# A two-layer graph network on one core: the first block's rows gathered from x during the prologue

## The chip, the core and the metric

The kernel runs on one core of one Trainium2 chip. The metric is the device time of one execution in microseconds; the median of several runs is compared. A core has five engines that run beside each other, each with its own queue: TensorE (PE in the profile, its weight loads PEld), VectorE (DVE), ScalarE (ACT), GpSimd (POOL) and SyncE (SP). SP issues most of the plain loads and stores here; GpSimd issues the gathers (indirect DMAs).

## What is computed

Two message-passing layers over a graph of 6250 nodes and 200000 edges, sorted by destination. `x` has 128 features per node. Cut to what matters:

```python
h = relu(layernorm(x))
z = h @ W                                   # 128 features, as 8 heads of 16
el, er = z . attn_l, z . attn_r             # per head
e = leaky_relu(el[src] + er[dst], 0.2)
a = exp(e - segment_max(e, dst)[dst])
x = x + segment_sum(z[src] * a, dst) / segment_sum(a, dst) + bias

h = relu(layernorm(x))
s, v = h[:, :32] @ W_up_s, h[:, 32:] @ W_up_v
w = silu(silu(edge_attr_8 @ A1 + b1) @ A2 + b2) @ A3
m = products of s[src], v[src], edge_attr_4 and w       # 256 per edge
x = x + (segment_sum(m, dst) / 10) @ W_out
```

What bears on the change is `z[src]` and `el[src]`: each edge needs a row of 136 values (128 of `z`, 8 of `el`) of its source node. `layernorm`, relu and the product with `W` act on each row by itself, so a row of the table can be made from a row of `x`, wherever that row has been copied to.

## The kernel before

**The edges.** The edges are cut into tiles of 128 (1563 of them), and 16 tiles (`KB`) make a block; there are 98 blocks (`NB`). A block's edges fall into a window of 128 nodes, so sums over edges are products with one-hot matrices on TensorE.

**The prologue** (L842 to L957) makes the table `t0` in DRAM: one row of 136 values per node. The nodes are 50 tiles of 128 rows, in ten chunks `gx` of 2, 3, 5, 6, 6, 6, 6, 6, 6 and 4 tiles. SP loads the ten chunks of x (`xs`, L865), then `src_col` (the source of every edge), `d_i` and `q_i` (destinations of every edge and of the edge before it) and `off`. Then a software pipeline steps over the chunks: `moments` (mean and variance on DVE, L814 and L816), `deviation` (a square root on ACT, L821), `normal` (DVE, L826 and L828), the normalized tile `fh` (L895 on ACT, L899 on GpSimd or DVE), a transpose on PE (L909), relu on ACT (`h_t`, L911), the product with `w_ext` (L917), a copy to `zt` on ACT, or on DVE for the last two chunks (L922), and `to_table` (L785 to L798), which stores `zt` to `t0` by SP. The last 8 columns of the product, `er`, are copied to `er_all` on GpSimd (L926). PE, DVE and ACT run in the order in which the program is written (`manual_schedule`); SP and GpSimd in an order that the scheduler chooses.

After the chunks GpSimd gathers the 16 tiles of block 0 from `t0` into `z_first` (L833). DVE checks that the edges are in order and evenly spread (L933 to L950) and leaves a number in `ok_i`; `er_all` is split into three bf16 parts `er3` (L953 to L957). Each engine then loads `ok_i` (L958) and takes one of two branches (L959): `even_edges`, which runs here, or a general kernel.

**The branch** loads constants and weights by SP (L990 to L1011), makes masks over the edges (L1014 to L1050: DVE, ACT, and five loads by SP), and then runs layer 0 as a loop over the blocks, with PE, DVE, ACT and SP in the written order. GpSimd issues 16 gathers for each block, or 15 where SP fetches the last tile row by row (L1078, every third block). The gathered block lies in one of five buffers `g` of the pool `fz`; `take_rows(g + 3)` asks for a block three steps before it is used, and a buffer comes back when the block's sums (L1234, PE) are done. Block 0 uses `z_first`. Layer 1 runs in the same way from a second table; its gathers have the same form.

Of the kernel before, what the change touches and what calls it, by code (L numbers as in the profile page):

```python
# [9 lines left out]
F32 = mybir.dt.float32  # L10
BF = mybir.dt.bfloat16
I32 = mybir.dt.int32
AF = mybir.ActivationFunctionType
OP = mybir.AluOpType
AX = mybir.AxisListType
PSUM = bass.MemoryType.PSUM
DRAM = bass.MemoryType.DRAM

P = 128
H = 8  # L20
D = 16
F = H * D
ZW = F + H
# [6 lines left out]
KB = 16  # L30
# [705 lines left out]
W0 = 32  # L736
# [5 lines left out]
def tile_even_edges(  # L742
# [46 lines left out]
    def to_table(table, of, i, n, eng):  # L789

        if i == 0:
            eng.dma_start(table[: P - W0, :], of[W0:, 0, :])
            if n > 1:
                to = table[P - W0 : n * P - W0]
                eng.dma_start(to.rearrange("(j p) f -> p j f", p=P), of[:, 1:n, :])
            return
        to = table[i * P - W0 : (i + n) * P - W0]
        eng.dma_start(to.rearrange("(j p) f -> p j f", p=P), of[:, :n, :])  # L798
# [20 lines left out]
    def deviation(pool, mv, n, name, m=P):  # L819
        rs = pool.tile([P, n, 1], F32, name=f"rs{name}")  # L820
        nc.scalar.activation(rs[:m], mv[:m, :, 1:2], AF.Sqrt, bias=eps[:m])  # L821
        return rs

    def normal(pool, mv, rs, n, name, m=P):

        nc.vector.reciprocal(rs[:m], rs[:m])  # L826
        mr = pool.tile([P, n, 1], F32, name=f"mr{name}")
        nc.vector.scalar_tensor_tensor(mr[:m], mv[:m, :, 0:1], -1.0, rs[:m], op0=OP.mult, op1=OP.mult)  # L828
        return rs, mr
# [8 lines left out]
    def tiles_of(a, first):  # L838
        return a[first : first + TG * P * P].rearrange("(g t e) -> t g e", t=P, e=P)


    with tc.manual_schedule(engines={mybir.EngineType.PE, mybir.EngineType.DVE,  # L842
                                     mybir.EngineType.Activation}), \
# [12 lines left out]
        w_ext = fx.tile([P, CW], F32, name="fw_ext")  # L856
# [9 lines left out]
        nc.sync.dma_start(src_col, srcc)  # L866
        d_i = fx.tile([P, TG, P], I32, name="fd_i")
        nc.sync.dma_start(d_i, tiles_of(dstt, P))
        q_i = fx.tile([P, TG, P], I32, name="fq_i")
        nc.sync.dma_start(q_i, tiles_of(dstt, P - 1))  # L870
        off = fx.tile([P, TG], F32, name="foff")
        nc.sync.dma_start(off, nums[:, NB * KB : NB * KB + TG])
# [7 lines left out]
        er_all = fx.tile([P, NX, H], F32, name="fer_all")  # L880
        NC = len(gx)
        mvs, rss, mrs, hs = {}, {}, {}, {}
        todo, done, outs = [], [], []
        for k in range(NC + 3):
            if 0 <= k - 1 < NC:
                rss[k - 1] = deviation(fp, mvs[k - 1], gx[k - 1][1], f"x{gx[k - 1][0]}")
            c = k - 2
            if 0 <= c < NC:
                i, n = gx[c]
                rs, mr = rss[c], mrs[c] = normal(fp, mvs[c], rss[c], n, f"x{i}")  # L890
                h = hs[c] = fp.tile([P, 10, P], F32, name="fh")
                for j in range(n):
                    by = (i + j) % 7
                    if by in ((2, 6) if c < NC - 2 else (2,)):
                        nc.scalar.activation(h[:, j, :], xs[c][:, j, :], AF.Identity,  # L895
                                             bias=mr[:, j, :], scale=rs[:, j, :])
                    else:
                        eng = nc.gpsimd if by in (0, 3, 5) and c < NC - 2 else nc.vector
                        eng.tensor_scalar(h[:, j, :], xs[c][:, j, :], mvs[c][:, j, 0:1],  # L899
                                          rs[:, j, :], op0=OP.subtract, op1=OP.mult)  # L900
            if k >= 3:
                i, n = gx[k - 3]
                zt = fp.tile([P, 10, CW], F32, name="zt")
                todo += [(k - 3, zt, j0, min(3, n - j0)) for j0 in range(0, n, 3)]
            while todo:
                c, zt, j0, m = todo.pop(0)
                p_t = fp_ps.tile([P, 4, P], F32, name="p_t")
                for j in range(m):
                    nc.tensor.transpose(p_t[:, j, :], hs[c][:, j0 + j, :], ident)  # L909
                h_t = fp.tile([P, 3, P], F32, name="h_t")  # L910
                nc.scalar.activation(h_t[:, :m], p_t[:, :m], AF.Relu)  # L911
                done.append((c, zt, j0, m, h_t))
                while len(done) > (1 if k < NC + 2 or todo else 0):
                    c, zt, j0, m, h_t = done.pop(0)
                    p_z = fp_ps.tile([P, 3, CW], F32, name="p_z")
                    for j in range(m):
                        nc.tensor.matmul(p_z[:, j, :], h_t[:, j, :], w_ext, start=True, stop=True)  # L917
                    outs.append((c, zt, j0, m, p_z))
                    while len(outs) > (1 if k < NC + 2 or todo or done else 0):
                        c, zt, j0, m, p_z = outs.pop(0)  # L920
                        copy = nc.scalar.copy if c < NC - 2 else nc.vector.tensor_copy
                        copy(zt[:, j0 : j0 + m, :], p_z[:, :m])  # L922
                        i, n = gx[c]
                        if j0 + m == n:
                            to_table(t0, zt[:, :, :ZW], i, n, nc.sync)
                            nc.gpsimd.tensor_copy(er_all[:, i : i + n, :], zt[:, :n, ZW:])  # L926
            if k < NC:
                i, n = gx[k]
                mvs[k] = moments(fp, xs[k], n, f"x{i}")
        gather(z_first, t0, range(KB), ZW)  # L930

        bad = fx.tile([P, TG, P], F32, name="fbad")
        nc.vector.tensor_tensor(bad, d_i, q_i, OP.is_lt)  # L933
        vs = fx.tile([P, 4], F32, name="fvs")
        nc.vector.tensor_reduce(vs[:, 0:1], bad.rearrange("p g e -> p (g e)"), AX.X, OP.add)
        w3 = fx.tile([P, 3, TG], F32, name="fw3")
        ef = fx.tile([P, 2, TG], F32, name="fef")
        nc.vector.tensor_sub(ef[:, 0, :], d_i[:, :, 0], off)
        nc.vector.tensor_sub(ef[:, 1, :], d_i[:, :, P - 1], off)
        nc.vector.tensor_single_scalar(w3[:, 0, :], ef[:, 0, :], 0.0, op=OP.is_lt)  # L940
        nc.vector.tensor_single_scalar(w3[:, 1, :], ef[:, 1, :], float(P), op=OP.is_ge)
        nc.vector.tensor_tensor(w3[:, 2, :], ef[:, 0, :], ef[:, 1, :], OP.is_equal)
        nc.vector.tensor_reduce(vs[:, 1:2], w3.rearrange("p a g -> p (a g)"), AX.X, OP.add)
        ones = fx.tile([P, 1], F32, name="fones")
        nc.vector.memset(ones, 1.0)
        p_v = fp_ps.tile([P, 4, P], F32, name="p_t")
        nc.tensor.matmul(p_v[:1, 0, :2], ones, vs[:, :2], start=True, stop=True)
        vr = fx.tile([1, 1], F32, name="fvr")
        nc.vector.tensor_reduce(vr, p_v[:1, 0, :2], AX.X, OP.add)
        nc.vector.tensor_copy(ok_i, vr)  # L950
# [14 lines left out]
def even_edges(tc, v):  # L965
# [5 lines left out]
    xp, dstc, y4, f8, bias, out, moments, deviation, normal, gather, tiles_of = (v[k] for k in (  # L971
        "xp", "dstc", "y4", "f8", "bias", "out", "moments", "deviation", "normal", "gather", "tiles_of"))
    with ExitStack() as ctx:
        const = ctx.enter_context(tc.tile_pool(name="fconst", bufs=1))
        z_pool = ctx.enter_context(tc.tile_pool(name="fz", bufs=5))
# [22 lines left out]
        wup = const.tile([P, P], F32, name="fwup")  # L998
        nc.sync.dma_start(wup, v["wup"])
        a1p = const.tile([P, KB // 2, P], F32, name="fa1p")  # L1000
        nc.sync.dma_start(a1p, v["a1p"])
        a2p = const.tile([P, P], F32, name="fa2p")
        nc.sync.dma_start(a2p, v["a2p"])
        a3p = const.tile([P, 2, P], F32, name="fa3p")
        nc.sync.dma_start(a3p, v["a3p"])
        b1 = const.tile([P, 1], F32, name="fb1")
        nc.sync.dma_start(b1, v["b1"])
        b2 = const.tile([P, 1], F32, name="fb2")
        nc.sync.dma_start(b2, v["b2"])
        wout = const.tile([P, 2, P], F32, name="fwout")  # L1010
        nc.sync.dma_start(wout, v["wout"])  # L1011
# [11 lines left out]
        with tc.tile_pool(name="fbuild", bufs=1) as build:  # L1023
            d_c = build.tile([P, TU], I32, name="fd_c")
            nc.sync.dma_start(d_c, dstc)
            d_i = build.tile([P, TG, P], I32, name="fd_i")
            nc.sync.dma_start(d_i, tiles_of(dstt, P))
            q_i = build.tile([P, TG, P], I32, name="fq_i")
            nc.sync.dma_start(q_i, tiles_of(dstt, P - 1))
# [20 lines left out]
            nc.sync.dma_start(t1z[LATE * P - W0 :].rearrange("(j p) f -> p j f", p=P), zeros)  # L1050

# [796 lines left out]
```

## Time and profile before

| | us |
|---|---|
| median of three runs | 3887.06 (3886.89 to 3891.37) |
| profiled execution | 3888.67 |
| its span | 3886.9 |
| busy: GpSimd | 2913.0 (75%) |
| busy: TensorE matmuls | 2848.8 (73%) |
| busy: VectorE | 2224.5 (57%) |
| busy: ScalarE | 1396.8 (36%) |
| first gather into `fz_first` | starts at 42.58 |
| first gather of the branch (block 1) | starts at 63.16 |

The span is the time from the first to the last record of the profiled execution; 1.8 us of its own time lie around it. A line of the profile's groups reads: line of the program, engine, operation, output and inputs by name, count, then the busy time with the mean of one, then the idle time just before these instructions and what ended most of it. In the timeline a row has its start and its duration in us, and in square brackets the idle time before it and what ended that. A queue of an engine (SPq, POOLq) is its sequencer, which issues DMAs, waits on semaphores and takes branches.

### The profile page before, as it was taken

How to read it: one execution, taken by the hardware profiler on the slowest of the kernel's cores; microseconds unless marked ns; L12 is line 12 of the kernel's file. 1: busy time of each engine (PE TensorE's matmuls, PEld its weight loads, DVE VectorE, ACT ScalarE, POOL GpSimd, SP SyncE). 2: the span in 40 equal slices, each digit the busy share in tenths (PEclk: the TensorE clock that was granted, in tenths of full speed). 3: DMA queues.
4: the chain of work that ended last, by engine and by line, in shares of the span. 5: the costliest groups of instructions: out<-in, count | busy, mean ns of one | idle time of the engine just before them, and what ended most of it. 6: DMA issues, size and time to landing. Idle time of an engine off the chain costs nothing. (4 is left out here: it accounts for less than half of the span.)

```text
span 3886.9 us, 62701 instructions
## 1 busy us (share of the span) xinstructions
PE 2848.8 (73%) x14785; PEld 2401.2 (62%) x14785; DVE 2224.5 (57%) x5408; ACT 1396.8 (36%) x3612; POOL 2913.0 (75%) x3096
## 2 busy tenths in 40 slices
PE   3766666666666766666678888888877777778777
PEld 3656656656556656666666666666666556656665
DVE  5544444444444444444457777677766666666666
ACT  3323232323322323232324444444444444444443
POOL 6777777777777777777777777777777777777776
PEclk6666666666666566666689999999999999999999
DMA  6222222222222222222222222222222222222221
GB/s 181 59 64 64 62 64 64 64 62 64 62 64 62 64 61 64 62 64 62 61 61 61 61 62 62 62 62 62 62 62 62 62 62 61 63 60 63 61 61 50
DMA packets 195262, 252.65 MB, mean 65 GB/s; under 512 B 78656, under 2 KB 145088, under 8 KB 194880
## 3 DMA queue, kind: packets, MB, share of 16 engines
q0 software_dynamic: 98048, 207.27, 22.6%
q1 hardware_dynamic: 96544, 41.19, 4.1%
q8 instruction: 120, 1.97, 0.2%
q14 instruction: 262, 2.15, 0.2%
q10 hardware_dynamic: 288, 0.07, 0.0%
HBM read 234.73 MB, written 13.25 MB: 64 GB/s over the span
## 5 line engine op out<-in xcount | busy, mean ns | idle before, releaser
L833 POOL DMA_INDIRECT g<-ft,fsrc x3024 | 2856.7, 945 | 922.4 <-issue 858.3
L1570 PE MATMUL p_u<-mj,s 128*128 128x256 f32 x3126 | 789.9, 397 | 217.9 <-DVE mj L1562 216.5
L1570 PEld LDWEIGHTS p_u<-mj,s 128*128 128x128 f32 x3126 | 588.9, 196 | 385.7 <-DVE mj L1562 310.9
L1234 PE MATMUL p_u<-g,s 128*128 128x136 f32 x3062 | 597.8, 376 | 0.4 <-DVE g L1229 0.4
L1234 PEld LDWEIGHTS p_u<-g,s 128*128 128x128 f32 x3062 | 572.1, 279 | 0.5 <-DVE g L1229 0.4
L1537 ACT ACTIVATE p_w<-p_w,yb 128x64 f32<-128x64 f32 x1563 | 450.3, 288 | 121.5 <-PE p_w L1533 80.4
L1553 DVE TENSOR_TENSOR vy<-g,p_i 128x384 f32<-128x384 f32 x387 | 212.9, 550 | 366.6 <-DMA g<-ft,fsrc 258.0
L1533 PE MATMUL p_w<-fa3p,h 128*128 128x256 f32 x1564 | 412.0, 387 | 0.0
L1151 PE MATMUL p_d<-fident,s 128*128 128x128 f32 x1563 | 384.7, 411 | 0.0
L1533 PEld LDWEIGHTS p_w<-fa3p,h 128*128 128x128 f32 x1564 | 289.4, 195 | 118.1 <-issue 52.5
L1176 DVE TENSOR_TENSOR e_s<-g,p_n 128x128 f32<-128x128 f32 x96 | 27.5, 286 | 578.6 <-DMA g<-ft,fsrc 566.2
L1518 ACT ACTIVATE h<-p_h,fb 128x512 f32<-128x512 f32 x196 | 134.6, 687 | 573.2 <-PE p_h L1516 571.8
L1151 PEld LDWEIGHTS p_d<-fident,s 128*128 128x128 f32 x1563 | 312.4, 225 | 37.6 <-issue 26.3
L1144 ACT COPY mk<-p_m 128x385 f32<-128x385 f32 (+1 forms) x99 | 47.6, 481 | 781.3 <-PE p_m L1141 781.2
L1229 DVE TENSOR_TENSOR g<-g,pe 128x1024 f32<-128x1024 f32 x193 | 225.5, 1209 | 129.2 <-ACT g L1220 126.4
L1153 ACT CAST d<-p_d 128x512 bf16<-128x512 f32 x391 | 228.8, 586 | 192.0 <-PE p_d L1151 141.6
L1179 PE MATMUL pe<-fident,e_s 128*128 128x128 f32 x98 | 39.1, 399 | 326.2 <-DVE e_s L1177 326.2
L1097 DVE TENSOR_TENSOR s<-p_n,fdloc 128x512 f32<-128x512 f32 x391 | 266.1, 682 | 6.7 <-ACT sv L1289 3.4
L1097 DVE TENSOR_TENSOR s<-p_i,fdloc 128x512 f32<-128x512 f32 x391 | 266.1, 681 | 3.8 <-ACT p_i L1512 3.8
L1516 PE MATMUL p_h<-ft,fa1p 128*128 128x128 f32 x1568 | 217.2, 283 | 63.3 <-DMA ft<-in_e_f_dram 63.1
L1516 PEld LDWEIGHTS p_h<-ft,fa1p 128*128 128x128 f32 x1568 | 210.6, 198 | 83.9 <-issue 65.3
L1523 ACT ACTIVATE h<-p_h,fb 128x512 f32<-128x512 f32 x196 | 134.7, 687 | 307.1 <-PE p_h L1520 307.1
(202 smaller groups left out, 3344.3 us busy)
## 6 DMA issues: line engine op xcount, KB each, us to landing
r<-ft SPq DMA_DIRECT2D x3968, 0.5 KB
r<-ft SPq DMA_DIRECT2D x3968, 0.5 KB
g<-ft,fsrc POOLq DMA_INDIRECT x3024
ft<-in_e_f_dram SPq DMA_DIRECT2D x98, 64.0 KB
yb<-in_e_y_dram SPq DMA_DIRECT2D x98, 32.0 KB
fx_all<-in_e_xp_dram SPq DMA_DIRECT2D x48, 64.0 KB
out_dram<-fx_all SPq DMA_DIRECT2D x47, 64.0 KB
ft<-sv SPq DMA_DIRECT2D x46, 64.0 KB
```

The costliest lines, as they stand in the source:

```text
L833: nc.gpsimd.indirect_dma_start(out=to[:, k, :width], out_offset=None, in_=table, in_offset=bass.IndirectOffsetOnAxis(ap=src_col[:, t : t + ...
L1097: nc.vector.tensor_tensor(s[:, :m], iota[:, None, :].to_broadcast([P, m, P]), dloc[:, t : t + m].unsqueeze(2).to_broadcast([P, m, P]), OP. ...
L1151: nc.tensor.transpose(p_d[:, k, :], c["s"][q][:, k, :], ident)
L1153: nc.scalar.copy(d[:, :m], p_d[:, :m])
L1229: nc.vector.tensor_mul(zh, zh, p_a[:, k0 : k0 + m].unsqueeze(3).to_broadcast([P, m, H, D]))
L1234: nc.tensor.matmul(c["p_u"][:, :ZW], c["s"][k // 4][:, k % 4, :], c["z"][:, k, :], start=c["o"] + k == 0, stop=c["o"] + k == KT[c["b"]] - 1)
L1516: nc.tensor.matmul(p_h[:, q, :], a1p[:, q0 + q, :], c["ft"], start=True, stop=True)
L1523: nc.scalar.activation(h2, p_h, AF.Silu, bias=b2)
L1533: nc.tensor.matmul(w[:, k : k + n].rearrange("p k a u -> p (k a u)"), c["h2"][q // 4][:, q % 4, :], a3p[:, :n].rearrange("p k f -> p (k f) ...
L1537: nc.scalar.activation(w[:, k, ::2, :], w[:, k, ::2, :], AF.Copy, scale=c["yb"][:, k0 + k, 0:1])
L1553: nc.vector.tensor_mul(vy, v_n, y_p)
L1570: nc.tensor.matmul(blk[b]["p_u"][:, :MW], u["s"][:, k, :], u["mj"][:, k, :], start=k0 + k == 0, stop=k0 + k == KT[b] - 1)
```

## The change

- The scheduler's freedom in the prologue ends: GpSimd and SP follow the written order too.
- GpSimd gathers 16 x 128 rows of `x` (not of the table) into `z_first` at the beginning of the prologue. Their indices are the first 16 columns of the sources, loaded by themselves as `src_0` on ACT's queue, plus 32 for the padding of `x`.
- The pipeline over chunks becomes a function `rows_of`. It is called a second time in the branch, after the masks, on `z_first` in chunks of 6, 6 and 4 tiles; there its result is written over `z_first` itself. The gathers of `z_first` from `t0` are gone. `w_ext` moves to the pool that outlives the prologue.
- In the prologue GpSimd normalizes only in chunks 6 and 7 (5 tiles; before, 17 tiles in all). The others go to DVE, and so do the copies to `er_all`.
- `off`, `d_i` and `src_col` are loaded later: after the store of chunk 1 (`off`, `d_i`) and of chunk 3 (`src_col`). One load with 129 values per row stands for `d_i` and `q_i`, here and in the branch. `zt` has four buffers of six tiles for three of ten.
- The check of the edges is cut in two: the comparisons run on DVE one step before the last chunk (`uneven_edges`), the count as bf16 products on PE with one reduction (`count_uneven`).
- In the branch the pool `fz` is opened before `fconst`, and the masks and the pass over `z_first` stand ahead of the loads of the weights of layer 1.

The diff, cut to its core:

```diff
@@ prologue
     with tc.manual_schedule(engines={mybir.EngineType.PE, mybir.EngineType.DVE,
-                                     mybir.EngineType.Activation}), \
+                                     mybir.EngineType.Activation, mybir.EngineType.Pool,
+                                     mybir.EngineType.SP}), \
...
-        w_ext = fx.tile([P, CW], F32, name="fw_ext")
+        src_0 = fx.tile([P, KB], I32, name="fsrc0")
+        nc.scalar.dma_start(src_0, srcc[:, :KB])
+        w_ext = keep.tile([P, CW], F32, name="fw_ext")
...
-        nc.sync.dma_start(src_col, srcc)
-        d_i = fx.tile([P, TG, P], I32, name="fd_i")
-        nc.sync.dma_start(d_i, tiles_of(dstt, P))
-        q_i = fx.tile([P, TG, P], I32, name="fq_i")
-        nc.sync.dma_start(q_i, tiles_of(dstt, P - 1))
-        nc.sync.dma_start(off, nums[:, NB * KB : NB * KB + TG])
+        def load(k):
+            if k == 1:
+                nc.sync.dma_start(off, nums[:, NB * KB : NB * KB + TG])
+                nc.sync.dma_start(d_i, with_before(dstt))
+            elif k == 3:
+                nc.sync.dma_start(src_col, srcc)
...
+        row_0 = fx.tile([P, KB], I32, name="frow0")
+        nc.vector.tensor_single_scalar(row_0, src_0, W0, op=OP.add)
+        for k in range(KB):
+            nc.gpsimd.indirect_dma_start(
+                out=z_first[:, k, :P], out_offset=None, in_=xp,
+                in_offset=bass.IndirectOffsetOnAxis(ap=row_0[:, k : k + 1], axis=0))
...
+        def uneven_edges():
+            nc.vector.tensor_tensor(bad, d_i[:, :, 1:], d_i[:, :, :P], OP.is_lt)
...
+        def count_uneven():
+            p_v = fp_ps.tile([P, 512], F32, name="p_v", bufs=1)
+            b = bad.rearrange("p g e -> p (g e)")
+            for k in range(0, TG * P, 512):
+                n = min(512, TG * P - k)
+                nc.tensor.matmul(p_v[:1, :n], ones, b[:, k : k + n], start=k == 0, stop=False)
+            nc.tensor.matmul(p_v[:1, : 3 * TG], ones, w3.rearrange("p a g -> p (a g)"),
+                             start=False, stop=True)
+            vr = fx.tile([1, 1], F32, name="fvr")
+            nc.vector.tensor_reduce(vr, p_v[:1, :], AX.X, OP.add)
+            nc.vector.tensor_copy(ok_i, vr)
+
+        def rows_of(gx, xs, raw, fp, fp_ps):
...
-                        eng = nc.gpsimd if by in (0, 3, 5) and c < NC - 2 else nc.vector
+                            late = by in (0, 3, 5) and NC - 4 <= c < NC - 2 and not raw
+                            eng = nc.gpsimd if late else nc.vector
...
+                if k == NC + 1 and not raw:
+                    uneven_edges()
+                for i, n, zt in ers:
+                    nc.vector.tensor_copy(er_all[:, i : i + n, :], zt[:, :n, ZW:])
+                ers = []
                 if k >= 3:
                     i, n = gx[k - 3]
-                zt = fp.tile([P, 10, CW], F32, name="zt")
+                    zt = z_first[:, i : i + n, :] if raw else fp.tile([P, 6, CW], F32, name="zt", bufs=4)
...
-                            to_table(t0, zt[:, :, :ZW], i, n, nc.sync)
-                            nc.gpsimd.tensor_copy(er_all[:, i : i + n, :], zt[:, :n, ZW:])
+                            if j0 + m == n and not raw:
+                                to_table(t0, zt[:, :, :ZW], i, n, nc.sync)
+                                ers.append((i, n, zt))
+                                load(c)
...
-        gather(z_first, t0, range(KB), ZW)
+        rows_of(gx, xs, "", fp, fp_ps)
+        count_uneven()
@@ even_edges
+        z_pool = ctx.enter_context(tc.tile_pool(name="fz", bufs=5))
         const = ctx.enter_context(tc.tile_pool(name="fconst", bufs=1))
-        z_pool = ctx.enter_context(tc.tile_pool(name="fz", bufs=5))
...
+        with tc.manual_schedule(engines={mybir.EngineType.PE, mybir.EngineType.DVE,
+                                         mybir.EngineType.Activation}), \
+                tc.tile_pool(name="fe", bufs=2) as fe, \
+                tc.tile_pool(name="fe_ps", bufs=2, space=PSUM) as fe_ps:
+            gz = [(k, min(6, KB - k)) for k in range(0, KB, 6)]
+            v["rows_of"](gz, [z_first[:, k : k + n, :P] for k, n in gz], "e", fe, fe_ps)
+
         wup = const.tile([P, P], F32, name="fwup")
         nc.sync.dma_start(wup, v["wup"])
...
```

## Prediction

> **What bounds the kernel now.** I read the page from its end backwards. The table of costliest groups comes first, then the chain of waits, then the timeline of GpSimd (POOL).
>
> ```profile
> L833 POOL DMA_INDIRECT g<-ft,fsrc x3024 | 2856.7, 945 | 922.4 <-issue 858.3
> ```
>
> 3024 gathers (3064 with the two sets into `fz_first`) of 945 ns. The idle time before them is called "issue": it waits for nothing. The timeline of POOL shows the period:
>
> ```profile
> 38.86 1.80 POOL L926 COPY fer_all<-zt 128x32 f32<-128x32 f32 x1 [0.95 <-DVE zt L922]
> 42.58 1.17 POOL L833 DMA_INDIRECT fz_first<-ft,fsrc  x1 [1.92 <-issue]
> 44.06 0.94 POOL L833 DMA_INDIRECT fz_first<-ft,fsrc  x1 [0.30 <-issue]
> ...
> 61.91 0.95 POOL L833 DMA_INDIRECT fz_first<-ft,fsrc  x1 [0.30 <-DMA fz_first<-ft,fsrc]
> 63.16 0.94 POOL L833 DMA_INDIRECT g<-ft,fsrc  x1 [0.30 <-DMA fz_first<-ft,fsrc]
> 64.41 0.95 POOL L833 DMA_INDIRECT g<-ft,fsrc  x1 [0.30 <-issue]
> ```
>
> One gather starts every 1.25 us. From 42.58, 3064 x 1.2485 = 3825 us brings the last gather's end to 3868; the trace has its last ones at 3867 to 3872, and none waits longer than 0.3 us for data or a buffer. So span = start of the stream (42.6) + 3064 periods + a tail of some 15 us. The chain of waits confirms the end of it:
>
> ```profile
> 3865.97 0.94 POOL g L833
> 3866.91 0.30 POOLq L1843
> 3867.21 3.72 DMA g<-ft,fsrc
> ```
>
> Only two things move the end: fewer gathers after the stream's start, or an earlier start. Everything on TensorE, VectorE (DVE) and ScalarE (ACT) counts only if it delays a gather. The prologue (0 to 42.58) shows what sets the start:
>
> ```profile
> 14.96 4.50 SPq L872 DMA_DIRECT2D foff<-in_e_nums_dram  x1
> 19.58 0.36 SPq L792 DMA_DIRECT2D ft<-zt  x1
> ```
> ```profile
> ACT zt L922 <- DMA ft<-zt: 4.3, 1, 4.3
> ```
>
> SP's queue is held up by the loads of `d_i`, `q_i` and `off`, so the first table store goes out at 19.58, and ACT waits 4.35 us (19.5 to 23.9) for a `zt` buffer.
>
> **What the Trainium skill says.** "GPSIMD Engine Reference", section 4, has GpSimd's own cores generate the descriptors of the DMAs issued through it: a gather costs engine time whatever the transfer does. The trace agrees: from 50 to 65 us the DMA share is 1.06 and the gathers still take 0.94. "SBUF — State Buffer", "SBUF: two separate sides", says that VectorE and GpSimd share a port pair under an exclusive lock. The trace agrees: beside DVE's 1.8 to 1.9 us mask operations (68.35 to 75.5) five gathers take 1.39 to 1.66, together 2.9 us more. "DMA: Bandwidth & Descriptors", "Anatomy of one DMA", gives about 2 us of fixed cost per DMA, mostly the receipt. Here the last table copy ends at 38.80 and the gather that needs it starts at 42.58: 3.78 us with issue and landing, which I use.
>
> **The change, part by part.**
>
> *Sixteen gathers leave the stream.* From 42.58 to 63.16 they cost 20.58 us. They now read `xp`, need only `src_0`, and run beside the loading. `src_0` goes out on ACT's queue at about 0.9; the weight load issued there at 0.91 was used at 3.69, so it lands near 3.3. `row_0` waits for it on DVE with all `bn_stats` behind it; the first of those started at 3.37 anyway, so 0.1 us is lost. `w_ext` and `att` are issued 0.4 us later; their first use for a table is at 9.6. The gathers run from 3.5 for 16 x 1.25 = 20, up to 16 x 1.66 = 27 at the slowest row shown, hence to 23.5 or 30. POOL's five normalizations for chunks 6 and 7 stand behind them; chunk 6 is due near 24.
>
> *Work moved from POOL to DVE in the prologue.* POOL had 17 normalizations and keeps 5; twelve at 0.27 on DVE are 3.2 us. Ten `er_all` copies: some 0.16 each, 1.6. The order check is moved ahead of the last copies: 1.88 plus five small ones, 2.5; the reduction of 1.89 becomes five matmuls. With `row_0` that is 7.4 us. DVE was busy about 24.5 us between 3.37 and the last `zt` copy's end, T = 38.8. With 7.4 more: 31.9, so T is 35.3 if DVE never idles; waits for x (0.8) and for the last products make 36.5. That is possible because ACT's 4.35 us go: the first two stores come ahead of `off` and `d_i`, one load replaces two, `src_col` follows chunk 3, and `zt` has four buffers. Bounds: 34.5 (only the stall goes) to 41.9 (stall gone, all 7.4 on the path). `off`, `d_i` (some 16 us now, wanted near 31) and `src_col` (near 24, wanted at 40) are hidden; at 300 GB/s each takes 3 us.
>
> *The branch is no longer hidden.* The sixteen gathers covered the check (`ok_i` ready at 43.80, five us after T), the load of the flag (0.5) and the branch: SP needed 1.06 us from flag to first instruction. Now POOL stands there. The table path gives T + 3.8 = 40.3. The check path: last matmuls 0.5, reduction 0.6, copy 0.15, flag and branch 1.1, so T + 2.4. The `er3` casts follow on DVE for 2.5 us; if the first buffer has to wait for that, 36.5 + 1.5 + 2.5 + 0.2 = 40.7. I take **first gather of the branch at 40.7** where 63.16 stood: 22.5 us. Bounds 38.3 to 45.7, which is 24.9 to 17.5.
>
> *The pass in the branch.* In the branch POOL never waits for this pass directly; what counts is when buffers come back. `fz` has five; block 6's first gather is the 80th in the branch, and needs block 1's sums. Those ended at 127.84; block 6 began near 164. Now it is due at 40.7 + 79 x 1.2485 + 2.9 = 142.2. When are the sums done? DVE's masks started at 68.35, 22.0 after SP's first load (46.36). From ahead of them go eight weight loads (4.1) and `q_i` (2.9), so they start at 40.2 + 15.0 = 55. They then take what they took. The pass stands after them: 16 tiles at the prologue's 0.7 us per tile (35.4 us for 50) and three steps of filling at 2.5, 18 us. Net: 55 + 18 - 68.35 = 4.9 us later, so sums at 132.7, and 9.5 us are spare. The weight loads now follow and are needed a node later, 70 us on; the single-row loads of SP start no later than before. Cost zero; bounds 0 to 10. Buffers after that gain 7 us a block, since a block's compute takes some 12 us beside 19.6 of gathers.
>
> *Contention.* The pass's normalizations on DVE, a dozen of 0.27, run beside gathers; 0 to 3 us by the mask rows above, I take 1.0. The swap of `fz` and `fconst` and the larger `keep` move addresses: 0, with either sign inside the bounds of the branch entry.
>
> **Sum.** The profiled execution took 3888.67 (span 3886.9, 1.8 around it): 3888.67 - 22.5 + 1.0 = 3867.2. It lies 1.6 above the median of 3887.06, so the forecast is 3865.6.
>
> **Rivals.** *A, the cover is short:* block 1's sums end 10 to 25 us later than before's, because the pass runs slowly beside TensorE at half clock (0.50 there). Each us beyond 142 is lost once: 1 to 15 us, 3867 to 3880. For it: the spare 9.5 is an estimate; against: DVE idles 18.5 us before the masks. *B, the prologue gives back:* the five normalizations behind slow gathers, and a late entry into the branch, put the first gather at 46 to 52: 3871 to 3877. *C, slower:* the same buffer, but the pass and block 0 are chained so that block 1's sums end after 163.7, 36 us later than before; from there the loss exceeds the 21.5 gained, and 175 would give 3898. It would take a pass of 50 us for 16 tiles, against 35 for 50 in the prologue. *D, no gain:* the early gathers are held until x is stored as a table, or block 1 waits for the pass; then the same 16 periods stand idle: 3887 plus or minus 5. The operands show no such dependence.
>
> **How the numbers follow.** Forecast 0.78, A 0.10, B 0.05, C 0.03, D 0.04. What a measurement here can tell from no change is about 0.2%, 7.8 us; the forecast, A and B lie beyond it: faster 0.93, same 0.04, slower 0.03. Range: low end 3887.06 - 24.9 = 3862; high end 3887.06 - 17.5 + 3 = 3873, which takes in half of A and B.
>
> **What would show it.** In the timeline of POOL after: sixteen gathers of `fz_first` between 3.5 and 30; the first `g` gather near 40.7; 1.25 us from there with no wait over 0.3 at blocks 6 and 7; no 4 us wait of ACT for `zt`. Wrong would be: a gap in POOL near 142 (A, C), a first `g` gather after 46 (B), or early gathers that start only near 40 (D).

## The result and the profile after

| | before | after |
|---|---|---|
| median of five runs, us | 3887.58 (3886.89 to 3891.37) | 3866.88 (3866.45 to 3867.51) |
| profiled execution, us | 3888.67 | 3867.01 |
| its span, us | 3886.9 | 3865.1 |
| first gather of the branch | 63.16 | 40.82 |
| first gather of layer 1 | 1959.38 | 1937.47 |

The ratio is 0.9944, with a 95% interval of 0.993 to 0.9959: 20.7 us faster, where 21.5 were forecast (3865.6). Below, "before" and "after" are the two kernels. In nine of the twelve experimental runs every kernel, the one before included, took about 6200 to 6330 us, with TensorE, VectorE and ScalarE standing still again and again for 10 us and more; these runs are called stalled, and of them I use the first part of the timeline and the differences between kernels, not the ratio as a verdict on the change.

In the groups of after, GpSimd's gathers are what they were, with as many of them; their idle time is 12 us more, which is the wait before the first:

```profile
L833 POOL DMA_INDIRECT g<-ft,fsrc x3024 | 2857.7, 945 | 934.4 <-issue 859.1
```

The timeline of GpSimd after (start, duration, engine, line, operation, operands, in brackets the idle time before):

```profile
3.77 1.09 POOL L899 DMA_INDIRECT fz_first<-in_e_xp_dram,frow  x1 [2.70 <-DVE stx L814]
5.17 0.96 POOL L899 DMA_INDIRECT fz_first<-in_e_xp_dram,frow  x1 [0.30 <-issue]
...
22.75 0.94 POOL L899 DMA_INDIRECT fz_first<-in_e_xp_dram,frow  x1 [0.30 <-issue]
24.15 4.21 POOL L951 TENSOR_SCALAR fh<-fxs,mvx,rsx 128x128 f32<-128x128 f32 x5 [0.46 <-PE p_t L966]
40.82 1.03 POOL L833 DMA_INDIRECT g<-ft,fsrc  x1 [12.46 <-DVE feq L1069]
42.15 0.95 POOL L833 DMA_INDIRECT g<-ft,fsrc  x1 [0.30 <-issue]
...
142.72 0.94 POOL L833 DMA_INDIRECT g<-ft,fsrc  x1 [0.30 <-issue]
```

The sixteen early gathers fill 3.8 to 23.7; the five normalizations stand right behind them (the last 0.46 us before them are a wait for TensorE, not for the gathers); then GpSimd waits 12.46 us. (The profile names a small DVE operation at the end of this wait; experiment 3 shows that it ends with the landing of the last table store.) From 40.82 to layer 1's end no gather waits longer than 0.3 us. The row at 142.72 is the first gather of block 6, where a late buffer would have shown. The chain of waits ends as before, in gathers and the landing of the last:

```profile
3847.93 0.30 issue
3848.23 0.95 POOL g L833
3849.18 0.30 issue
3849.48 2.83 DMA g<-ft,fsrc
```

The last gather starts 21.5 us earlier than in before (3870.95), and the span is 21.8 shorter. So the gain exists at 40.8 us into the kernel (22.3 us there) and is carried through, but for 0.9 us.

### The profile page after: what moved, and what is told of

It reads as the page before. It is cut to its first block, busy times and chain, and to the rows that moved or that the text cites. A ratio compares the mean times of both kernels' runs of the same rounds, so it can differ in the third digit from the quotient of the medians.

```text
span 3865.1 us, 62861 instructions
## 1 busy us (share of the span) xinstructions
PE 2825.6 (73%) x14836; PEld 2380.3 (62%) x14836; DVE 2237.5 (58%) x5485; ACT 1403.0 (36%) x3625; POOL 2900.2 (75%) x3074
## 3 DMA queue, kind: packets, MB, share of 16 engines
q1 hardware_dynamic: 93184, 39.50, 3.9%
## 5 line engine op out<-in xcount | busy, mean ns | idle before, releaser
L1286 PE MATMUL p_u<-g,s 128*128 128x136 f32 x3062 | 588.1, 372 | 1.0 <-DVE g L1281 0.4
L1286 PEld LDWEIGHTS p_u<-g,s 128*128 128x128 f32 x3062 | 563.2, 276 | 1.7 <-DVE g L1281 1.6
L1203 PE MATMUL p_d<-fident,s 128*128 128x128 f32 x1563 | 370.6, 400 | 0.9 <-DVE s L1149 0.9
L1203 PEld LDWEIGHTS p_d<-fident,s 128*128 128x128 f32 x1563 | 300.7, 218 | 11.6 <-DVE s L1149 1.1
```

The costliest lines, as they stand in the source:

```text
L1203: nc.tensor.transpose(p_d[:, k, :], c["s"][q][:, k, :], ident)
L1286: nc.tensor.matmul(c["p_u"][:, :ZW], c["s"][k // 4][:, k % 4, :], c["z"][:, k, :], start=c["o"] + k == 0, stop=c["o"] + k == KT[c["b"]] - 1)
```

## Experiments

The theory: the end is set by the stream of gathers alone. The gain is the sixteen gathers that left it and its earlier start. The pass in the branch is free because the buffers of blocks 6 and 7 come back in time. The rivals: the new order of loads brings most of it; the pass is hidden wherever it stands, or costs its full length.

### 1. The new loads alone

```diff
-            nc.gpsimd.indirect_dma_start(out=z_first[:, k, :P], ..., in_=xp, ...)
...
+        gather(z_first, t0, range(KB), ZW)
...
-            v["rows_of"](gz, [z_first[:, k : k + n, :P] for k, n in gz], "e", fe, fe_ps)
```

> The changed kernel without its early gathers and without its pass in the branch: block 0's rows are gathered from the table once it is stored, as before the change; the new prologue (order of loads, check cut in two, fewer operations on GpSimd) stays. My theory (the 16 gathers that leave the stream carry the gain): the first z_first gather starts near 40 instead of 42.6, the first g gather near 60.5 instead of 63.2, and the time is some 2.5 us under the kernel before, about 3885. Rival (the restructured prologue carries the gain, the early gathers would have been hidden anyway): about 3867, as the changed kernel.

The same kernel again, twice:

> The same kernel as e1_table_gathers, once more, since in that comparison every kernel, the one before the change included, stood still for up to 20 us at a time and took some 6300 us. Where the kernel before takes some 3887 us again: my theory (the 16 gathers that leave the stream carry the gain) 3884 to 3886, first z_first gather near 39.5; rival (the restructured prologue carries it) 3866 to 3868.

> The edit: the changed kernel's new order of loads, without the gathers from x and without the pass over their rows; block 0's rows come from the table as before. Theory (the gain is the 16 gathers that leave the stream plus the stream's earlier start): GpSimd's stream starts at 39.3 instead of 42.6, so 3.3 us of the 20.7 are there and the time is 3884.3 within 1; the 16 gathers carry the other 17.5. Rival (the new loads bring most of it, the early gathers little): 3870 or less.

Medians were 6302.45, 6214.59 and 6296.79, the ratios 0.9994 (0.9981 to 1.0007), 0.9989 (0.998 to 0.9998) and 0.9995 (0.9983 to 1.0007). All three runs were stalled, so the expected 3884 was never measured. But up to the first stall the timeline can be read. That of GpSimd in the second of them:

```profile
39.27 1.16 POOL L833 DMA_INDIRECT fz_first<-ft,fsrc  x1 [12.43 <-DMA ft<-zt]
...
62.48 0.95 POOL L833 DMA_INDIRECT g<-ft,fsrc  x1 [0.30 <-issue]
```

The stream starts at 39.27 (39.30 and 39.72 in the others) where before it was 42.58: the new prologue gives 3.3 us. (Before itself was not profiled in a stalled run.) The 12.43 us before the row end with the store of the table. So the rival, that the new loads bring most of the gain, falls by the timeline and not by the time. Block 1's first gather stands at 62.48, in which 3.0 us are gathers stretched by the masks, which now fall among these sixteen; in before and after they fall behind. The split of the gain in GpSimd's stream is then: 3.3 us from the earlier start, 20.2 from sixteen periods gone, minus 1.55, because after's stream starts at 40.82 and not at 39.27. That is 21.95, and layer 1's first gather moved by 21.91.

The 1.55 us are not the price of entering the branch. They stand in the prologue, as the last store of the table shows, in this kernel and in after:

```profile
34.72 0.37 SPq L798 DMA_DIRECT2D ft<-zt  x1
```
```profile
36.24 0.37 SPq L798 DMA_DIRECT2D ft<-zt  x1
```

From this store to the first gather behind it are 4.55 us here and 4.58 in after, through the branch. The first store of the table is late by as much (14.50 here, 16.03 in after), so the loss arises in the first microseconds; its place is shown below, in the part on the prediction.

### 2. The early gathers with the old loads

```diff
+        nc.sync.dma_start(src_col, srcc)
+        nc.sync.dma_start(d_i[:, :, 1:], tiles_of(dstt, P))
+        nc.sync.dma_start(q_i, tiles_of(dstt, P - 1))
+        nc.sync.dma_start(off, nums[:, NB * KB : NB * KB + TG])
         def load(k):
...
```

> The changed kernel with the loads of the prologue as before the change: src_col, d_i, q_i and off right behind x on SP's queue, ahead of every table store. My theory (the first g gather of the branch starts when the prologue ends, and the late stores hold it up): first table store again near 19.6 instead of 16.0, ACT or DVE wait for zt up to 4 us, the first g gather 1 to 4 us later than 40.8, and the time 1 to 4 us longer than the changed kernel, 3868 to 3871. Rival (the four zt buffers and the slack of DVE swallow the late stores): the same as the changed kernel within 0.5 us, 3866.4 to 3867.4.

6307.92, ratio 1.0013 (1.0002 to 1.0023). Inconclusive: the first table store went out at 27.68 and the first gather of the branch at 51.72, but the prologue was stretched in the other stalled runs with early gathers too (the next experiments), whatever their loads. This run is used below as one with one pass.

### 3. The pass left out, once, twice

Without the pass (block 0's rows stay those of x, and their `el` is zero):

```diff
-            v["rows_of"](gz, [z_first[:, k : k + n, :P] for k, n in gz], "e", fe, fe_ps)
+        nc.vector.memset(z_first[:, :, P:], 0.0)
```

> The changed kernel without the pass over z_first in the branch: block 0's messages are computed from raw rows of x and zeros, so its output is not the reference's. My theory (the pass is hidden behind gathers; of it only its contention with the gathers is on the path): block 1's sums end some 12 to 16 us sooner than 132.6, and the time falls by 0 to 1 us, 3866 to 3867. Rival (the pass is partly on the path, because buffers come back late somewhere in layer 0): 2 us or more off, under 3865.

And with the pass twice:

```diff
             v["rows_of"](gz, [z_first[:, k : k + n, :P] for k, n in gz], "e", fe, fe_ps)
+            v["rows_of"](gz, [z_first[:, k : k + n, :P] for k, n in gz], "f", fe, fe_ps)
```

> The changed kernel with the pass over z_first run twice (the second run on the result of the first, so block 0's messages are not the reference's). My theory (the cover is the five buffers of fz: block 6's first gather is due at 142.3 and needs block 1's sums, which end at 132.6 in the changed kernel): the second pass takes 14 to 16 us more, the sums end near 148, GpSimd waits 4 to 7 us near 142 and nowhere else in layer 0, and the time is 3871 to 3874. Rival (the buffers are not the limit, the compute of layer 0 catches up without holding GpSimd): 3867. Second rival (each us of the pass beyond one pass is on the path): 3882.

> The same kernel as e4_pass_twice (the pass over z_first run twice, block 0's messages not the reference's), once more for the same reason. Where the kernel before takes some 3887 us again: my theory (five buffers of fz are the cover; some 9.7 us of it are spare) a wait of GpSimd of 4 to 7 us near 142 and 3871 to 3874; rival (compute catches up without holding GpSimd) 3867; second rival (every us of the pass is on the path) 3882.

> The edit: the pass over the 16 early tiles runs twice, one behind the other, its statistics, matmuls and copies and all. Theory (the pass is free only as long as block 1's sums end ahead of block 6's first gather, 132.6 against 142.3 in the changed kernel): the second pass adds its 16 us, block 1's sums end near 149, GpSimd stands still once, for 6 to 8 us, at block 6's first gather, with PE p_u named, and the time is 3873 to 3875. Rival 1 (the pass is hidden wherever it stands): 3867 and no gap. Rival 2 (the pass is on the path in full): 3883.

> The edit: the pass over the 16 early tiles runs twice, one behind the other, its statistics, matmuls and copies and all; the second takes the rows that the first made for rows of x, so block 0's values are not the reference's. Theory (the pass is free only as long as block 1's sums end ahead of block 6's first gather, 132.6 against 142.3 in the changed kernel): the second pass adds its 16 us, block 1's sums end near 149, GpSimd stands still once, for 6 to 8 us, at block 6's first gather, with PE p_u named, and the time is 3873 to 3875. Rival 1 (the pass is hidden wherever it stands): 3867 and no gap. Rival 2 (the pass is on the path in full): 3883.

The first three runs of the doubled pass, and the one without it, were stalled. In one comparison the medians are 6291.84 without the pass and 6325.18 with it twice, 33.3 us apart: 16.7 for each pass, about its length (16.0 in after), with some 6 us either way by the intervals. The kernel of experiment 2, with one pass but also with the old loads, lies between them at 6307.92. The ratios are 0.9990 (0.9981 to 1.0000), 1.0046 (1.003 to 1.0063) and 1.0013 as above; the doubled pass gave 1.0027 (1.0013 to 1.004) and 1.004 (1.0025 to 1.0054) in two other comparisons. What the engines waited for, from the table of waits of the kernel without the pass (us in all, times, longest):

```profile
ACT h L1570 <- remote: 801.7, 81, 15.4
ACT d L1200 <- remote: 752.0, 117, 19.0
```

"Remote" is what the profile names when another core or a queue that it doesn't know ends a wait; before and after show no such row. There the computing sets the end, GpSimd is busy 46% and waits for buffers from block 6 on:

```profile
192.41 0.94 POOL L833 DMA_INDIRECT g<-ft,fsrc  x1 [39.99 <-PE p_u L1281]
```

So where gathers are not the bound, the times fit Rival 2's price, the full length of the pass. My expectations for these runs came from the wrong bound.

The fourth run of the doubled pass was not stalled (before beside it: 3890.93). It took 3877.76 (3875.7 to 3879.64), ratio 0.9967 (0.9955 to 0.9978). The gain over before shrinks from 20.7 to 13.2: the second pass costs 7.5 us, where the theory said 6 to 8, Rival 1 none and Rival 2 sixteen. Its timeline of GpSimd has exactly these waits over 0.36 us behind the first gather of the branch:

```profile
142.09 0.95 POOL L833 DMA_INDIRECT g<-ft,fsrc  x1 [0.30 <-issue]
147.58 0.94 POOL L833 DMA_INDIRECT g<-ft,fsrc  x1 [4.54 <-PE p_u L1287]
...
165.06 0.94 POOL L833 DMA_INDIRECT g<-ft,fsrc  x1 [0.30 <-issue]
170.00 0.94 POOL L833 DMA_INDIRECT g<-ft,fsrc  x1 [4.00 <-issue]
...
174.02 0.95 POOL L833 DMA_INDIRECT g<-ft,fsrc  x1 [0.58 <-issue]
```

and TensorE's timeline of the same run the sums that they wait for:

```profile
142.86 3.95 PE L1287 MATMUL p_u<-g,s 128*128 128x136 f32 x32
...
167.22 2.02 PE L1287 MATMUL p_u<-g,s 128*128 128x136 f32 x16
```

Block 1's sums end at 146.81 and block 6's first gather follows at 147.58, 4.24 us beyond its period. Block 2's sums end at 169.24 and block 7's first gather follows at 170.00, 3.7 us beyond; 0.28 more at 174.02. "Once, for 6 to 8 us" was therefore wrong: it is twice, 8.2 in all. The profile calls the second wait "issue", but it ends 0.76 us after the sums, as the first does (0.77). Compared with after, the last gather starts 11.67 us later: 1.08 in the first gather of the branch (41.90), 8.22 in the gaps, and 2.37 spread evenly over both layers, a slower pace that before shows beside it too (3.35 us longer than above). That is why the time missed 3873 to 3875 though the price of the pass was right.

This run also settles what starts the branch. The casts to `er3` ended at 39.50 (39.61 in after), but the queues of SP and GpSimd, both inside the branch by then, were released by the landing of the last table store at 40.68 (39.59 in after). The first gather came 1.22 us after that landing, in after 1.23. In after the two stood 0.02 us apart; here they are 1.18 apart, and the gather that starts the stream follows the table and not the casts. SP's waits show the same late landing (us in all, times, longest), first in after, then here:

```profile
SPq L1034 <- DMA ft<-zt: 1.0, 1, 1.0
```
```profile
SPq L1034 <- DMA ft<-zt: 2.1, 1, 2.1
```

The second gap has a cause that I had not seen. ScalarE's timeline in this run:

```profile
151.66 0.30 ACT L1145 COPY g<-r 128x136 f32<-128x136 f32 x1 [8.97 <-DMA r<-ft]
```

It waits 8.97 us for the row-by-row tile of block 3, and block 2's sums start 9.3 us behind that copy (161.00). In after it is the same 9.3 us: copy at 136.09, sums at 145.43. So block 2's sums stand behind SP's single-row loads; experiment 4, where these start earlier, agrees.

### 4. The pass and the row offsets ahead of the masks

```diff
+        at = [const.tile([P, P], I32, name=f"fat{i}") for i in range(2)]
+        ...
+            v["rows_of"](gz, [z_first[:, k : k + n, :P] for k, n in gz], "e", fe, fe_ps)
         d_c = build.tile([P, TU], I32, name="fd_c")
...
-            v["rows_of"](gz, [z_first[:, k : k + n, :P] for k, n in gz], "e", fe, fe_ps)
...
-        at = [const.tile([P, P], I32, name=f"fat{i}") for i in range(2)]
```

> The edit: inside the branch, the pass over the rows gathered early and the row offsets stand ahead of the masks; gathers and prologue stay as in the changed kernel. Theory (the order of these is off the path, since blocks 1 to 5 have buffers of their own): first gather of the branch at 40.8 within 0.5, SP's single-row loads start near 60 and not at 86, ScalarE's two waits of 10 us for them are gone, block 1's sums end 10 to 20 us before 132.6, and the time stays within 2 us of the changed kernel's 3866.9. Rival (block 6's buffer is nearer to its due time than the trace says): the earlier sums bring 2 us or more. Where every kernel takes about 6200 because the engines stand still for other reasons, the start of the branch alone is to be read.

3867.66 (3866.67 to 3868.18), before in the same comparison 3887.7, ratio 0.9949 (0.9933 to 0.9966). From its timelines of SP, ScalarE and TensorE:

```profile
61.40 18.65 SPq L1132 DMA_DIRECT2D r<-ft  x49
```
```profile
111.75 0.30 ACT L1146 COPY g<-r 128x136 f32<-128x136 f32 x1 [1.59 <-DMA r<-ft]
164.03 0.30 ACT L1146 COPY g<-r 128x136 f32<-128x136 f32 x1 [3.48 <-DMA r<-ft]
```
```profile
110.33 3.95 PE L1288 MATMUL p_u<-g,s 128*128 128x136 f32 x32
```

Every internal point came as expected: the rows start at 61.4, the waits of 10 us are gone, block 1's sums end at 114.28 and not at 132.64. Block 2's sums end at 128.05 and not at 153.1. And the time does not move. Eighteen us of earlier sums are worth nothing, since the gathers of blocks 6 and 7 already found their buffers free. The theory holds; the rival (2 us or more) falls.

### 5. Nine gathers more

```diff
+                if c == NC - 3 and not raw:
+                    for q in range(NA):        # NA = 9, tiles of block 1
+                        nc.gpsimd.indirect_dma_start(out=z_second[:, q, :P], ..., in_=xp, ...)
```

With the pass over 25 tiles ahead of the masks, as in experiment 4:

> The edit: nine tiles of the second block are gathered in the prologue too (right behind GpSimd's five normalizations), their rows are made in the same pass, and the pass and the row offsets stand ahead of the masks. Theory (the stream of gathers from the first table gather to layer 1 has no gap, and each gather ahead of it is worth its 1.25 us once): the first gather of the branch still starts at 40.8 to 41.5, the early gathers fill about 11 of the 12.5 us of GpSimd's wait, block 6's first gather starts near 131 (9 x 1.25 earlier than 142.3), and on a chip where the kernel before takes 3887 the time falls by 11 more, to about 3856. Rival (the early gathers push back the last store of the table, or the buffers become the bound): first gather of the branch at 44 or later, or a gap at block 6 or 7; the time stays at 3862 to 3870. Where the engines stand still for other reasons and every kernel takes about 6200, neither shows in the time, and the start of the branch alone is to be read.

With the pass left behind the masks:

> The edit: nine tiles of block 1 are gathered in the prologue too, as in the kernel that reached 3856.6, but the pass over the now 25 tiles stays behind the masks, where the change has it. Theory (what is taken off the front of the stream is only worth its time while the sums come in time for the buffers): the first gather of the branch starts at 40.6 to 41, but the pass is 9 us longer, block 2's sums end near 162, block 7's first gather would be due near 150, GpSimd stands still there for about 12 us, and the time is 3866 to 3869, no better than the changed kernel. Rival (order in the branch is off the path here too): no gap, and 3856 as with the pass ahead of the masks.

The first took 3856.56 (3856.07 to 3857.45), before in the same comparison 3887.7, ratio 0.9921 (0.9905 to 0.9938). It beats both kernels. The fair partner is the kernel of experiment 4, with the same order in the branch and in the same comparison: 11.1 us less, and layer 1's first gather 10.9 earlier (1927.20 against 1938.11), where nine periods are 11.2. Against after it is 10.3 us, since with the pass ahead the gathers beside the masks are stretched by 4.2 us (experiment 4) and 4.5 (here), in after by 3.2. Its timeline of GpSimd:

```profile
23.71 4.08 POOL L953 TENSOR_SCALAR fh<-fxs,mvx,rsx 128x128 f32<-128x128 f32 x5
27.96 1.03 POOL L957 DMA_INDIRECT fz_second<-in_e_xp_dram,frow  x1 [0.16 <-issue]
...
31.82 1.77 POOL L957 DMA_INDIRECT fz_second<-in_e_xp_dram,frow  x1 [0.30 <-issue]
...
38.88 0.98 POOL L957 DMA_INDIRECT fz_second<-in_e_xp_dram,frow  x1 [0.30 <-issue]
40.63 0.94 POOL L835 DMA_INDIRECT fz_second<-ft,fsrc  x1 [0.77 <-issue]
```

The nine stand where after has its wait of 12.46 us; of that 0.77 is left, and the branch begins no later (40.63). This is the cleanest test of the price of one gather: the same stretch of idle time, filled, gives 1.21 to 1.23 us for each.

The second kernel took 6308.86, ratio 1.0018 (0.9999 to 1.0037), in a stalled run. It says nothing on the question whether the order in the branch matters there. That it would, as in experiment 3, is argued and not shown.

## Why the prediction was right

- **The bound.** One stream of gathers without gaps, whose start and count set the end: shown by the 21.9 us that are there at layer 1's first gather and by experiments 3 to 5. Of the 3064 gathers 32 are the two sets into `fz_first`; eight more are block gathers of layer 1 (`ft1z`).
- **Sixteen gathers.** "GPSIMD Engine Reference", section 4, of the Trainium skill has GpSimd's own cores make the descriptors of a gather. From this the prediction took that a gather costs engine time whatever the transfers do; after agrees again, with 0.94 us for nearly all early gathers at a DMA share of 1.01 (5 to 23 us). They were put at 3.5 to 23.5 and came at 3.77 to 23.69.
- **The start: the number was right, and partly by luck.** The first gather of the branch was put at 40.7 and came at 40.82. The prediction had it wait for the `er3` casts, 0.4 us behind the table. It waits for the table, and from the last `zt` copy to the gather it is 4.6 us and not 3.8. That copy ended at 36.2 (36.5), from two errors that cancel: DVE was busy for 30.0 us on the way (31.9) and idle for 2.8 (1.2). "The branch is no longer hidden" is not borne out as a price: see experiment 1.
- **What was wrong: the loads behind `src_0`.** "`w_ext` and `att` are issued 0.4 us later; their first use for a table is at 9.6" put this at nothing. But their first use is the product of `att` and the transpose of `w_ext`, behind which ScalarE's first square root stands in the written order, and VectorE waits for that root. In before:

```profile
4.49 0.61 PE L878 MATMUL p_t<-fatt,fw_t 128*128 128x16 f32 x2 [0.36 <-ACT fw_t L876]
5.21 0.48 ACT L821 ACTIVATE rsx<-mvx,feps 128x2 f32<-128x2 f32 x2
```

And in after:

```profile
6.16 0.58 PE L894 MATMUL p_t<-fatt,fw_t 128*128 128x16 f32 x2 [1.20 <-DMA fatt<-in_e_attn_dram]
6.84 0.48 ACT L821 ACTIVATE rsx<-mvx,feps 128x2 f32<-128x2 f32 x2
7.17 0.17 DVE L826 RECIPROCAL rsx<-rsx 128x2 f32<-128x2 f32 x1 [1.62 <-ACT rsx L821]
```

The root comes 1.63 us later. In the kernel of experiment 1, which has no `src_0`, it stands at 5.21 as in before. These are the 1.55 us of experiment 1. Why `att`, issued 0.48 us later, landed later by more than that is not shown, and no run with another order of these loads was made.
- **The cover: right, but its sum was lucky.** Masks at 54.49 (55). The pass took 16.0 us (18), but waited 5.56 for ScalarE's masks first. VectorE's first one-hot matrices of the loop therefore came at 84.67, 9.2 us later than before's 75.47, where 4.9 were forecast. Block 1's sums still ended at 132.64 (132.7), because VectorE's next wait, for TensorE, was 5.6 us in place of 10.2:

```profile
126.25 6.39 PE L1286 MATMUL p_u<-g,s 128*128 128x136 f32 x32
```

With 0.77 us from sums to gather, seen in experiment 3, the spare at block 6 was 142.72 - 0.77 - 132.64 = 9.3 us (9.5). The doubled pass moved block 1's sums by 14.2 and cost 4.24 there.
- **Contention: the sum was near, its place was wrong.** 1.0 was charged to the pass beside the gathers. From the first gather of the branch to layer 1 0.4 us were given back (22.34 became 21.91), and 0.4 more in layer 1. But no gather beside the pass (67.25 to 83.13) took more than 0.95, so the pass cost nothing that their durations show. The gathers beside the masks were stretched by 3.2 us, against 2.3 before (the prediction read five rows and 2.9 us; before has four such rows); half of these 0.9 us came back elsewhere. "SBUF — State Buffer", section "SBUF: two separate sides", of the Trainium skill has VectorE and GpSimd share a port pair under an exclusive lock; the stretched rows fit that, but no run here separates it from another cause. The longest of them in after:

```profile
54.63 2.56 POOL L833 DMA_INDIRECT g<-ft,fsrc  x1 [0.30 <-issue]
```

- **What was wrong: the single-row loads.** "The single-row loads of SP start no later than before" failed. Their addresses `fat` are computed by DVE and PE, and these now stand behind the pass. From the timeline of SP before, then from those of SP and ScalarE after:

```profile
70.93 4.13 SPq L1078 DMA_DIRECT2D r<-ft  x11
```
```profile
86.01 59.01 SPq L1130 DMA_DIRECT2D r<-ft  x152
```
```profile
136.09 0.30 ACT L1144 COPY g<-r 128x136 f32<-128x136 f32 x1 [10.02 <-DMA r<-ft]
```

SP's rows are 15 us late. ScalarE then waits 72.2 us for such rows over the whole run, in 19 waits, against 3.6 before. In after this costs nothing: block 2's sums (`151.08 2.02` in the timeline of PE) end at 153.1 and block 7's first gather is due at 161.4 (fifteen gathers behind 142.72), 7.6 us of spare. With 16 us more it cost 4.0, the second gap of experiment 3. The prediction counted one buffer's spare and got the right answer with the second unexamined, which is luck.
- **What was wrong: the offset.** 1.6 us were subtracted because before's profiled execution lay above its median. After's lies 0.13 from its median, and before's five runs spread over 4.5 us, so the shift looks like scatter. Without it the forecast is 3867.2 against 3866.88.
- **Small slips in its sums.** The pass was 16 x 0.7 + 3 x 2.5 = 18.7 us, not 18; 55 + 18 - 68.35 is 4.65, not 4.9; and sums 10 to 25 us late would lie at most 11 us beyond 142, not 15 (Rival A). None of them decides anything.

## What to carry to other kernels

Where one engine's queue has no gap, find a wait in that same queue and move work into it: here each gather moved into idle time was worth 1.2 to 1.25 us, and both the gap and the price could be read off the timeline beforehand. Price a load that is put in front of others on a queue by the first use of the loads behind it and by all that stands behind that use in written order: 0.4 us of issue became 1.5 us of prologue here. Work that this pushes onto other engines is free only up to the time when the first reused buffers are due, so compute due time minus ready time for each buffer in the first round, and list what else was standing behind the place where the new work is put. Then ask which bound the cover assumes: the pass that was free behind the gathers cost about its whole length where the computing set the end.

## What was not expected of the hardware

- The same kernels took 3857 to 3891 us in some comparisons and about 6200 to 6330 in others. It is not shown to be a property of the chip: the record has chip 0 both in a stalled comparison (the second run of experiment 1) and in one that was not (experiments 4 and 5). ScalarE's waits named "remote" were up to 19 us long in the rows shown, 800 us in all before one line. What held the engines is not shown by any run. It went together with gathers: in the second run of experiment 1 TensorE was busy for 4.9 of the 50 us from 100 to 150, with 40 gathers, and for 20.3 of the next 50, with nine; in after, with 40 gathers in each, it was 35.6 and 29.6.
- Every stalled run with early gathers had its five GpSimd normalizations near 34 to 35 and the first gather behind the table at 51 to 56, against 24 and 41 to 42 elsewhere; the three runs of experiment 1, without early gathers, had the normalizations at 23. Early gathers and the stretched prologue go together there; the cause stays open.
- A gather next to a VectorE mask operation of 1.9 us lasted up to 2.56 us, where before showed 1.66 at most. The sum over the gathers stretched beside the masks was 2.3 us in before, 3.2 in after, and 4.2 and 4.5 with the pass ahead of the masks. Why it differs is not shown.
